# A fused attention and experts kernel: where half of a key's product stands, and which engine makes the second batch's x sums

## The chip, the cores and the metric

The kernel runs on one core of a Trainium2 chip, in one launch. The metric is the device time of that core in microseconds (us). Engines are named as the profile names them: PE is the tensor engine (PEld its loading of weights), DVE the vector engine, ACT the scalar engine, POOL is GpSimd, SP the engine that issues nearly all DMAs. Everything is computed in fp32.

## The reference

The input x is 2 batches of 2048 tokens with 512 features. One layer of gated delta-rule attention with 16 heads of 128, and a mixture of experts on the first 512 rows:

```python
q = silu(conv4(x @ Wq)); k = silu(conv4(x @ Wk)) * 128 ** -0.5; v = silu(conv4(x @ Wv))
alpha = sigmoid(x @ Wa + ba); beta = sigmoid(x @ Wb + bb)
def step(S, (qt, kt, vt, at, bt)):                      # per token and head
    err = S @ kt - vt
    S = at * S - bt * outer(err, kt)
    return S, S @ qt
o = layernorm(scan(step)) * ln_w + ln_b
attn = (o * sigmoid(x @ Wg)) @ Wo
# experts: 16 of them, 4 per token, weighted and added
expert = (silu(x @ gate.T) * (x @ up.T)) @ down.T
```

conv4 is a causal convolution over four tokens, one filter per feature. Both parts read the layer norm of the input, and the output is the input plus both.

## The kernel before

**Units and blocks.** The work is cut into 16 units u: batch u // 8 and one pair of heads. A unit runs over 4 blocks of 512 tokens, each of 4 chunks of 128. Inside a chunk the recurrence is solved with the inverse of a triangular matrix, whose small pieces come from an "inverse" per unit (L251 to L282; its steps are two operations each, L268 and L271): it loads a tile Y, works in it, copies to a tile X and stores both. Tiles X and Y are one buffer each.

**Seven products instead of eight.** Projections of the recurrence use sums of quarters of x and of the weights, so that seven products of half size do for eight. The sums of x are made once per block by `combine` (L526 to L545): four subtractions of 128x512 on DVE, and seven stores of 256 KB into `xs_d`. `x_part` (L790 on) loads them back as tiles `xr`, and the products are at L821.

**First stage** (to about 233 us). It normalises x, transposes it, makes the decays (`zaz`, alpha and beta), the keys of unit 0 and the first of unit 1, the routing of the experts and inverse 0. The order on PE, DVE, ACT and POOL is the order in which the code is written; SP's DMAs are placed by the scheduler. Ahead of a loop the first batch is handled; sixteen memsets on POOL (L438 and L439) zero operand tiles at the very start. The loop (t from 3) then does, for t = 3 to 10, two chunks of the second batch each:

- `turned` (L492 to L506), twice: four PE transposes of 128x128 (L505) and one ACT copy (L506);
- `gated` (L508 to L516): PE products for the gates (L513) and an ACT copy into zr (L516);
- `spread` (L518 to L524): two small transposes (L523) of zr;
- `scaled` (L482 to L490): the normalisation of the next two chunks, on ACT for the second batch (L486); `moments` (L463 to L480): statistics on DVE and a power on POOL (L476);
- every second time `combine(1, g)`, with its sums on DVE.

Between these stand the steps of a pipeline of keys, one key (a head of a block) per t. `key_item` (L399 to L422) has the product in two halves (`proj_part`, L184, two matmuls of 128x512 each), the copy into `raw` and the last tap on ACT (`conv_taps`, L148 to L160), three taps on DVE (`conv_sum`, L166), and silu on ACT (L420). Behind the second half of a unit's last key the weights of the next unit are asked for (`load_wk`). Scores of older keys (`scores`, L228), their decays (`dec_start` L211, `dec_run` L219) and `put_a` (L232) follow. The routing (`route`, L1633 to L1687) gives steps in some turns of the loop.

```python
if first:
    turned(1, n1)
...
key_step(t), key_step(t)
if first:
    gated(1, n1)
```

**Recurrence** (`recurrence(b)`, L1106 on). For every chunk the code writes out a hand-made order: products of the next block's q, v, g and k, the chunk's own work, and the experts' work, whose gathers (L1696) are issued by POOL. POOL also makes the next unit's inverse, three steps in every chunk, from chunk 2 of a unit's first block on. Behind inverses 2 to 5, in u = 1 to 4, it makes sums of the output weights, `wo_sums` (L1248 to L1268): loads into tile Y, four subtractions of 128x256, two stores, twice in a unit. Everything on POOL runs in order, also L995 and L997 (the chunk's kv path), L920 (qg, 128x512) and L1080 and L1081 (rs and nb of the output norm), for which ACT's L1094 waits.

Of the kernel before, what the change touches and what calls it, by code (L numbers as in the profile page):

```python
# [45 lines left out]
def block_kernel(ctx, tc, x, wq, wk, wv, wg, wo, wa, wb, ba, bb, par, consts,  # L46
# [59 lines left out]
            for p in range(3)]  # L106


    xs_d = [[dp.tile([P, 7, 2 * TH], F32, name=f"xs_d{b}_{k}") for k in range(NBK)] for b in range(NB)]

    a_d = [dp.tile([H, NC * DW], F32, name=f"a_d{b}") for b in range(NB)]
    gin_d = [dp.tile([H, T], F32, name=f"gin_d{b}") for b in range(NB)]
# [322 lines left out]
             for k, n in (("a32", C), ("ilo", Q), ("ihi", C), ("top", 3 * Q), ("bot", C), ("a64", C))}  # L435
            for i in range(2)]
    invs = [opp.tile([P, HG, C], F32, tag=f"inv{i}", name=f"inv_{i}") for i in range(4)]
    for t in [*ops[0].values(), *ops[1].values(), *invs]:  # L438
        nc.gpsimd.memset(t, 0.0)  # L439

    with ExitStack() as es:
        mp = es.enter_context(tc.tile_pool(name="moe", bufs=2))
# [83 lines left out]
        def combine(b, g):  # L526

            if b > 0:
                first, second = xts[b, g * CB], xts[b, g * CB + 2]
            else:  # L530
                first, second = x0[g][:, :, 0:TH], x0[g][:, :, TH:]
            b11, b21, b12, b22 = first[:, 0:2], first[:, 2:], second[:, 0:2], second[:, 2:]
            eng = nc.vector

            def new():
                return bp.tile([P, 2, TH], F32, tag="v", name="t", bufs=4)

            t1, t2, t4 = new(), new(), new()
            eng.tensor_tensor(t1, b12, b11, ALU.subtract)
            eng.tensor_tensor(t2, b22, t1, ALU.subtract)  # L540
            eng.tensor_tensor(t4, b21, t2, ALU.subtract)
            t3 = b12 if b > 0 else new()
            eng.tensor_tensor(t3, b22, b12, ALU.subtract)
            for i, t in enumerate((b11, b21, t2, t1, t3, t4, b22)):
                nc.sync.dma_start(out=xs_d[b][g][:, i, :].rearrange("p (k t) -> p k t", k=2), in_=t)  # L545
# [102 lines left out]
        with tc.manual_schedule(engines={E.PE, E.DVE, E.Activation, E.Pool}):  # L648
            moments(0, 0, 1), moments(0, 1, 2)
            for g in range(NBK):  # L650
                for c in range(g * CB, (g + 1) * CB):
                    scaled(0, c)
                    if c + 2 < NC:
                        moments(0, c + 2, c + 3)
                    if c % 2 and g + 2 < NBK:
                        fetch(0, g + 2, (c % CB // 2,))
                    turned(0, c)
                    if c > 1:
                        (spread(0, c - 3) if c > 2 else None) if c % 2 else gated(0, c - 2)
                if g == 1:  # L660
                    key_step(0), key_step(0)
                if g > 1:
                    combine(0, g - 2)
                if g == 2:
                    key_step(0)
            gated(0, NC - 2)
            nc.vector.tensor_scalar(lnh, prm[:, 3 * H * (KS + 1):], 0.5, None, ALU.mult)
            d0, d1 = decays(0), decays(1)
            fetch(1, 0), fetch(1, 1)
            combine(0, 2)  # L670
            key_step(1)
            spread(0, NC - 2)
            next(d0)
            key_step(1), key_step(2), key_step(2)
            moments(1, 0, 2)
            next(d0), next(d0)
            ask(0, 0, 0), ask(0, 0, 1)
            key_step(1)
            key_step(0)
            next(d0), next(d0)  # L680
            key_step(2)
            drain(d0)
            scaled(1, 0), scaled(1, 1)
            key_step(1), key_step(0)
            combine(0, 3)
            moments(1, 2, 4)
            n1 = 0
            r = route(nc, any_bank, mp, cst, cstf[:, N_CONST * P:], topk_idx, topk_w, tw, pos, wrow, trow)
            inv, firsts = iter(()), []
            def first_inverse():  # L690
                yield from inverses(0, nc.vector)
                load_ops(0)

            for t in range(3, len(keyed) + 2):
                first = t < 11
                old = t - 3
                if t == 11:
                    loads(0)
                    firsts = [item(0, what, h, later)
                              for what, h in (("q", 0), ("v", 0), ("q", 1), ("v", 1), ("g", 0), ("g", 1))]  # L700
                if t == 11:
                    inv = first_inverse()
                    next(inv)
                p = firsts[t - 11] if 0 <= t - 11 < 6 else iter(())
                p1 = firsts[t - 12] if 0 <= t - 12 < 6 else iter(())

                if first:
                    turned(1, n1)
                done = keyed[old][0] < 2
                if done:  # L710
                    dec = dec_start(*keyed[old])
                key_step(t - 2)
                if done:
                    pk = bank(ps_l, "l") if old < 8 else any_bank()
                    scores(pk, kts.pop(keyed[old]))
                if first:
                    turned(1, n1 + 1)
                else:
                    next(d1, None)
                key_step(t), key_step(t)  # L720
                if first:
                    gated(1, n1)
                next(p, None), next(p, None)

                key_step(t - 1)
                if done:
                    dec_run(dec, *keyed[old])
                    put_a(pk, dec, *keyed[old])
                key_step(t)
                next(p1, None), next(p1, None)  # L730
                next(p, None)
                if first:
                    spread(1, n1)
                    n1 += 2
                    nxt = n1 // CB + 1
                    if n1 < NC:
                        scaled(1, n1), scaled(1, n1 + 1)
                    if n1 + 2 < NC:
                        moments(1, n1 + 2, n1 + 4)
                    if n1 % CB == 0:  # L740
                        combine(1, n1 // CB - 1)
                    if n1 % CB and nxt + 1 < NBK:
                        fetch(1, nxt + 1)
                for _ in range({4: 1, 5: 1, 6: 2, 7: 1, 8: 1, 9: 1, 10: 2}.get(t, 0)):
                    next(r)
                for _ in range(8):
                    next(inv, None)
                next(p1, None)
                saves()
            drain(d1, r, inv)  # L750
# [355 lines left out]
    def recurrence(b, pending):  # L1106
# [20 lines left out]
        with tc.manual_schedule(engines={E.PE, E.DVE, E.Activation, E.Pool}):  # L1127
# [8 lines left out]
            for m, at in enumerate([*steps, None, None]):  # L1136
# [4 lines left out]
                if at:  # L1141
# [10 lines left out]
                    if c == 2 and blk == 0:  # L1152
                        drain(inv)
                        inv = inverses(u + 1, nc.gpsimd) if u + 1 < NB * NP else none
                        if 0 < u <= H // 4:
                            inv = chain(inv, wo_sums(2 * u - 2, 2 * u - 1))
                        step(inv)
                    a = before(n, c)
                    what = (PLAN if n + 1 != n0 + (NP - 2) * NBK else "qvgk")[c]
# [88 lines left out]
    def wo_sums(*rows):  # L1248

        for i in rows:  # L1250
# [15 lines left out]
            nc.sync.dma_start(out=wo_d[:, 0, i, :], in_=t)  # L1266
            nc.sync.dma_start(out=wo_d[:, 1:, i, :], in_=w[:, 1:])
            yield  # L1268

    def chain(*gens):  # L1270
        for g in gens:
# [542 lines left out]
```

## Time and profile before

| | |
|---|---|
| median of 3 runs | 3609.84 us (3609.67 to 3609.89) |
| the profiled execution's own time | 3617.36 us |
| its span, first to last instruction | 3615.6 us |
| mean granted clock of PE | 0.989 |
| busy PE, DVE, ACT, POOL | 97%, 71%, 57%, 59% |
| moved by DMA | 714.60 MB |
| first product of the recurrence (L821) starts | 232.93 us |

The profiled execution took 7.52 us more than the median of the runs, so times from its trace add up to 3617.36 and not to 3609.84. PE is busy in 97% of the span, and the chain that ended last runs through PE for 83% of it. An average over the span hides the first stage: there PE is busy in 12 to 19 of every 20 us. "Granted clock" is the share of full speed that PE's throttle allowed. In a row of a timeline the number in brackets is the engine's idle time ahead of the instruction, with what ended it.

### The profile page before, as it was taken

Reading aid. Unit: us, or ns where it says so; the run is one execution under the profiler, and the core shown is the slowest. Engines: PE = TensorE matmul, PEld = TensorE weight load, DVE = VectorE, ACT = ScalarE, POOL = GpSimd, SP = SyncE. Lnnn points to the kernel's source line nnn. Section 1 sums busy time; section 2 is a strip of 40 time slices with the busy share of each in tenths; the row PEclk is TensorE's granted clock in tenths of the full one; section 3 lists DMA queues with packets and bytes.
Section 4 is the critical chain, followed back from the end, with each engine's and each line's share of the span. In section 5 each row is a group of like instructions: output and inputs, shape, how many; then the busy total and the mean of one; then the engine's idle time right before and its main releaser. Section 6 shows DMA issues by size and latency. Waiting matters only on the chain.

```text
span 3615.6 us, 69975 instructions
## 1 busy us (share of the span) xinstructions
PE 3500.4 (97%) x21604; PEld 3122.7 (86%) x21604; DVE 2562.0 (71%) x6468; ACT 2063.2 (57%) x5491; POOL 2127.2 (59%) x3680
## 2 busy tenths in 40 slices
PE   7889999999999999999999999999999999999999
PEld 4459888888888888889898889999999999899888
DVE  7777766767776777678784368888888888667532
ACT  4556555555655565666671047777767777666410
POOL 2137768677785777768661047666675858484200
PEclk9999999999999999999999999999999999999999
DMA  8667767768677687777787547575757576654432
GB/s 278 214 182 216 240 186 246 207 200 262 193 244 213 190 268 192 245 209 235 207 240 235 158 131 202 155 212 163 211 170 213 160 205 170 196 169 146 143 111 90
DMA packets 675652, 714.60 MB, mean 198 GB/s; under 512 B 364304, under 2 KB 469008, under 8 KB 675280
## 3 DMA queue, kind: packets, MB, share of 16 engines
q1 hardware_dynamic: 653168, 628.71, 59.5%
q0 software_dynamic: 22112, 81.41, 7.2%
q8 instruction: 175, 2.87, 0.3%
q14 instruction: 197, 1.61, 0.2%
HBM read 504.72 MB, written 205.13 MB: 196 GB/s over the span
## 4 chain that ended last, share of the span: by engine, by line
PE 83%; DMA 4%; DVE 3%; POOL 2%; ACT 2%; issue 1%; SPq 0%; POOLq 0%; DVEq 0%; ACTq 0%
PE y L821 21%; PE z L821 16%; PE z L1318 5%; PE p L1730 4%; PE l L967 3%; PE p L1318 3%; PE y L1318 3%; PE c L1049 3%; PE c L1040 3%; PE o L1064 3%; PE o L1067 3%; PE c L1029 3%; PE p L228 2%; PE p L1747 2%; PE l L1000 2%; PE l L982 2%
## 5 line engine op out<-in xcount | busy, mean ns | idle before, releaser
L911 DVE SCALAR_TENSOR_TENSOR cv<-raw,prm,cv 128x512 f32<-128x512 f32 x1086 | 934.4, 870 | 11.6 <-ACT cv L149 4.7
L995 POOL COPY inv<-iT 32x32 f32<-32x32 f32 x512 | 195.9, 383 | 378.0 <-DVE top L988 205.6
L826 ACT COPY e<-y 128x256 f32<-128x256 f32 x734 | 271.1, 369 | 240.2 <-PE y L821 233.7
L1080 POOL TENSOR_TENSOR rs<-rs,mhalf 128x2 f32<-128x2 f32 x256 | 181.6, 710 | 381.9 <-DVE nb L1079 379.4
L149 ACT ACTIVATE cv<-raw,prm 128x512 f32<-128x512 f32 x362 | 295.7, 817 | 108.1 <-DVE raw L887 108.1
L271 POOL TENSOR_TENSOR Y<-Y,t 128x30 f32<-128x30 f32 (+14 forms) x450 | 296.0, 658 | 35.2
L268 POOL TENSOR_TENSOR t<-Y 128x30 f32<-128x30 f32 (+14 forms) x450 | 280.1, 622 | 36.6 <-DMA gin<-gin_d 14.3
L1056 DVE SCALAR_TENSOR_TENSOR S<-S,gtot,c 128x128 f32<-128x128 f32 x480 | 145.0, 343 | 177.4 <-PE c L1049 176.9
L887 DVE TENSOR_TENSOR raw<-z,e 128x256 f32<-128x256 f32 x244 | 103.5, 424 | 230.1 <-PE z L821 229.0
L1102 ACT ACTIVATE oT<-c,lnh 128x256 f32<-128x256 f32 x256 | 144.2, 563 | 179.5 <-PE c L1099 168.8
L920 POOL TENSOR_TENSOR qg<-q,gin 128x512 f32<-128x512 f32 x126 | 192.2, 1525 | 72.2 <-DMA gin<-gin_d 46.7
L1094 ACT ACTIVATE o<-o,nb,rs 128x128 f32<-128x128 f32 x512 | 202.4, 444 | 45.3 <-POOL nb L1081 44.1
L821 PE MATMUL y<-xr,wq 128*128 128x256 f32 x756 | 197.7, 385 | 15.8 <-DMA xr<-xs_d 15.5
L1103 POOL TENSOR_TENSOR oT<-g,oT 128x256 f32<-128x256 f32 x256 | 192.0, 750 | 29.0 <-ACT oT L1102 28.6
L821 PE MATMUL y<-xr,wg 128*128 128x256 f32 x760 | 196.6, 381 | 5.7 <-DMA xr<-xs_d 5.7
L1064 PE MATMUL o<-w,pT 128*128 128x128 f32 x1024 | 194.8, 275 | 0.0
L821 PE MATMUL y<-xr,wv 128*128 128x256 f32 x756 | 194.5, 380 | 0.0
L1730 PE MATMUL p<-xgT,w 128*128 128x128 f32 x1488 | 181.4, 275 | 11.8 <-DVE aTf L232 7.5
L843 DVE TENSOR_TENSOR raw<-z,e 128x256 f32<-128x256 f32 x245 | 102.8, 420 | 123.5 <-ACT e L826 39.6
L1067 PE MATMUL o<-S,qg 128*128 128x128 f32 x960 | 185.7, 275 | 0.0
L1064 PEld LDWEIGHTS o<-w,pT 128*128 128x128 f32 x1024 | 173.3, 191 | 12.8
L1730 PEld LDWEIGHTS p<-xgT,w 128*128 128x128 f32 x1488 | 171.4, 182 | 14.5 <-DVE aTf L232 9.0
(335 smaller groups left out, 10187.6 us busy)
## 6 DMA issues: line engine op xcount, KB each, us to landing
xr<-xs_d SPq DMA_DIRECT2D x191, 512.0 KB
row<-a_d SPq DMA_DIRECT2D x128, 258.0 KB
dec_d<-decA SPq DMA_DIRECT2D x128, 258.0 KB
decB<-dec_d SPq DMA_DIRECT2D x64, 516.0 KB
gin<-gin_d SPq DMA_DIRECT2D x128, 256.0 KB
k_d<-kf SPq DMA_DIRECT2D x128, 256.0 KB
k<-k_d SPq DMA_DIRECT2D x64, 512.0 KB
aT_d<-aTf SPq DMA_DIRECT2D x128, 256.0 KB
```

Source lines behind the costliest of these rows:

```text
L149: nc.scalar.activation(cv, of, AF.Identity, bias=cbias(p, h0 + h), scale=tap(p, h0 + h, KS - 1))
L268: eng.tensor_tensor(t, bass.AP(col.tensor, col.offset, [col.ap[0], (Q, j), (0, n)]), bass.AP(row.tensor, row.offset, [row.ap[0], (0, j), ( ...
L271: eng.tensor_tensor(Y[:, 0:j, j + 1:], Y[:, 0:j, j + 1:], t, ALU.add)
L821: nc.tensor.matmul(ps[:, 0:TH], lhsT=a[i - 1][:, k, :], rhs=xs[j][:, slot, k, :], start=start and k == 0, stop=k == 1, skip_group_check=no ...
L826: nc.scalar.copy(e, py[:, 0:TH])
L911: nc.vector.scalar_tensor_tensor(cv, (r0, r1)[h][:, j:j + BLK], tap(p, u % NP * HG + h, j), cv, ALU.mult, ALU.add)
L995: nc.gpsimd.tensor_copy(inv[0:Q, h, Q:2 * Q], iT[r + Q:r + 2 * Q])
L1064: nc.tensor.matmul(po[:, h * D:(h + 1) * D], lhsT=pT[:, h, :], rhs=w[:, h, :], start=True, stop=S is None)
L1067: nc.tensor.matmul(po[:, h * D:(h + 1) * D], lhsT=qg[:, h, cs], rhs=S[:, h, :], start=False, stop=True)
L1094: nc.scalar.activation(o[:, h, :], po[:, h * D:(h + 1) * D], AF.Identity, bias=nb[:, h:h + 1], scale=rs[:, h:h + 1])
L1318: nc.tensor.matmul(ps[:, 0:TH], lhsT=a[0][h // 4][:, h % 4, :], rhs=W[w][h], start=start and h == 0, stop=h == n8 - 1, skip_group_check=no ...
L1730: nc.tensor.matmul(ps[:fn, s, :], lhsT=w[f][:, s, k, :], rhs=xt[:, k, :], start=(k == 0), stop=(k == NKT - 1))
```

## The change

Four edits go together.

1. `xs_d` of the second batch gets an eighth slot, and `combine(1, g)` only stores the four quarters of x, without sums: b11 in slot 0, b21 in slot 1, b12 in slot 7, b22 in slot 6.
2. A new `x_sums` makes the sums later, in the recurrence of the first batch, on POOL: it loads slots 0 and 1 into a tile of tag X and slots 6 and 7 into one of tag Y (512 KB each), lets three steps go by, subtracts four times and stores slots 2 to 5. It runs behind inverse 1 (blocks 0 and 1, in u = 0) and behind inverse 2 (blocks 2 and 3, in u = 1). The sums of the output weights move from u = 1 to 4 to u = 2 to 5.
3. The sixteen memsets move from the start to a place behind the first batch's last `combine` and `moments(1, 2, 4)`.
4. For t = 3 to 10 the first half of key t's product goes in front of the first `turned`, the second half behind the second `turned`; for later t the order stays.

```diff
-    xs_d = [[dp.tile([P, 7, 2 * TH], F32, name=f"xs_d{b}_{k}") for k in range(NBK)] for b in range(NB)]
+    xs_d = [[dp.tile([P, 7 + b, 2 * TH], F32, name=f"xs_d{b}_{k}") for k in range(NBK)] for b in range(NB)]
...
-    for t in [*ops[0].values(), *ops[1].values(), *invs]:
-        nc.gpsimd.memset(t, 0.0)
...
                 first, second = xts[b, g * CB], xts[b, g * CB + 2]
-            else:
-                first, second = x0[g][:, :, 0:TH], x0[g][:, :, TH:]
+                for t, lo in ((first[:, 0:2], 0), (first[:, 2:], 1), (second[:, 0:2], 7), (second[:, 2:], 6)):
+                    nc.sync.dma_start(out=xs_d[b][g][:, lo, :].rearrange("p (k t) -> p k t", k=2), in_=t)
+                return
+            first, second = x0[g][:, :, 0:TH], x0[g][:, :, TH:]
...
-            t3 = b12 if b > 0 else new()
+            t3 = new()
...
             moments(1, 2, 4)
+            for t in [*ops[0].values(), *ops[1].values(), *invs]:
+                nc.gpsimd.memset(t, 0.0)
...
                 if first:
+                    key_step(t)
                     turned(1, n1)
...
-                key_step(t), key_step(t)
+                key_step(t)
                 if first:
                     gated(1, n1)
+                else:
+                    key_step(t)
...
-                        if 0 < u <= H // 4:
-                            inv = chain(inv, wo_sums(2 * u - 2, 2 * u - 1))
+                        if u < 2:
+                            inv = chain(inv, x_sums(2 * u), x_sums(2 * u + 1))
+                        elif u < 6:
+                            inv = chain(inv, wo_sums(2 * u - 4), wo_sums(2 * u - 3))
...
+    def x_sums(blk):
+
+        lo, hi = (ap.tile([P, 2, 2, TH], F32, tag=tag, name="xh") for tag in "XY")
+        of = xs_d[1][blk]
+        for t, k in ((lo, 0), (hi, 6)):
+            nc.sync.dma_start(out=t, in_=of[:, k:k + 2, :].rearrange("p s (k t) -> p s k t", k=2))
+        for _ in range(3):
+            yield
+        b11, b21, b22, b12 = lo[:, 0], lo[:, 1], hi[:, 0], hi[:, 1]
+        nc.gpsimd.tensor_tensor(b11, b12, b11, ALU.subtract)
+        yield
+        nc.gpsimd.tensor_tensor(b12, b22, b12, ALU.subtract)
+        yield
+        nc.gpsimd.tensor_tensor(b22, b22, b11, ALU.subtract)
+        yield
+        nc.gpsimd.tensor_tensor(b21, b21, b22, ALU.subtract)
+        for k, t in enumerate((b22, b11, b12, b21)):
+            nc.sync.dma_start(out=of[:, 2 + k, :].rearrange("p (k t) -> p k t", k=2), in_=t)
+        yield
```

## The prediction

> **What bounds the kernel now.** I read the busy line of the page first, then a table of busy time by stretches, then the tensor engine's timeline where that table shows gaps.
>
> ```profile
> PE 3500.4 (97%) x21604; PEld 3122.7 (86%) x21604; DVE 2562.0 (71%) x6468; ACT 2063.2 (57%) x5491; POOL 2127.2 (59%) x3680
> ```
>
> The span is 3615.6 us, so PE idles 115 us in all. The stretches (columns: busy us of each engine, granted clock, DMA share, GB/s) tell where:
>
> ```profile
> core 0: us, PE busy (x) PEld busy (x) DVE busy (x) ACT busy (x) POOL busy (x), PEclk, DMA share, GB/s
> ...
> 80.00:100.00 20.00, 17.49 (x73) 10.54 (x70) 15.86 (x34) 11.47 (x24) 3.22 (x8) 0.91 0.88 288
> 100.00:120.00 20.00, 14.80 (x65) 8.92 (x65) 18.98 (x42) 11.47 (x24) 3.36 (x6) 0.91 0.92 293
> 120.00:140.00 20.00, 16.00 (x63) 9.05 (x62) 13.93 (x24) 10.12 (x22) 3.35 (x7) 0.87 0.70 202
> ...
> 220.00:240.00 20.00, 12.29 (x55) 9.29 (x55) 12.56 (x18) 8.20 (x23) 7.27 (x11) 0.83 1.01 319
> ...
> 420.00:440.00 20.00, 20.00 (x125) 17.43 (x124) 15.93 (x40) 12.85 (x31) 11.65 (x22) 1.00 0.74 178
> ```
>
> In the first stage (to 233 us) no engine is full: PE 14.8 to 17.5 of 20, and POOL, with 3, nearly free. In the recurrence PE is full (20.00 of 20), so there only a new PE wait costs. PE's timeline shows one period of the loop over t (start, duration, line, operation, and in brackets the idle time before it and its cause):
>
> ```profile
> 126.41 0.66 PE L505 MATMUL c<-unit,xn 128*128 128x128 f32 x4 [1.55 <-ACT xn L486]
> 126.90 1.06 PE L228 MATMUL l<-kf 128*128 128x128 f32 x8
> 127.79 1.02 PE L505 MATMUL c<-unit,xn 128*128 128x128 f32 x4
> 128.60 4.92 PE L184 MATMUL p<-x,wk 128*128 128x512 f32 x8
> 133.45 1.92 PE L513 MATMUL l<-xt,wab 128*32 128x256 f32 x8
> 135.82 0.31 PE L523 MATMUL o<-unit,zr 32*128 32x32 f32 x2 [0.45 <-ACT zr L516]
> 137.67 0.77 PE L505 MATMUL c<-unit,xn 128*128 128x128 f32 x4 [1.54 <-ACT xn L486]
> ```
>
> PE and ACT take turns: after `gated` (L513) PE waits 0.45 us for zr and 1.55 for xn, while ACT runs zr 0.36, the key's raw copy 0.57, cv 0.77 and xn 0.75. Undisturbed periods are 9.57 us (74.08 to 83.65, 94.76 to 104.33): 5.35 from transposes to `gated`, 1.91 of `gated`, 2.31 of ACT.
>
> **The change part by part.** *Half product in front.* Two of the four matmuls of 128x512 (half of 3.60 us: 1.8) come before the transposes, and 0.45+1.55 = 2.0 us of idle time can hold them. ACT's chain then sets the head of the next period at 2.6 after `gated`'s end; from there `gated` starts after 3.55 (two transposes, scores, the other half, ACT's copies), then 1.91: 8.06 instead of 9.57, or 1.5 less. Period by period, each by the head (first L505) before and worked out after:
> - t=3 and 4 (60.81, 74.08, 83.65): 1.5 each, 0 if something else holds.
> - t=5 (83.65 to 94.76): routing matmuls of 1.8 us fill part of the gap: 0.8 (0 to 1.55).
> - t=6: key 7 takes the bank that the routing holds until a DVE copy (L1652, ended 105.89), some 8.5 after the head; its half product must wait: 0.8 lost.
> - t=7: key 8 begins unit 1, whose weights are fetched only behind key 7's second half. That load was issued at 112.71 and landed at 118.5; PE waited 1.20 for it. In front of the transposes it is needed sooner: head after 11.6 instead of 9.57, 2 lost (0.2 to 2.1).
> - t=8 (12.51 long, with that 1.20 and slow-clock matmuls): 3.5 gained (2.7 to 4.4). t=9 (11.26): 2.6 (2.0 to 3.2). t=10, head 137.67 to `gated` 144.67: 2.7 (1.95 to 3.45).
>
> Sum 9.8 (6.5 to 14). The spread is the clock: the scores (L228) take 1.06 or 1.91 us, and the 100 to 140 us rows grant 0.91 and 0.87.
>
> Behind the gaps the granted clock falls: 0.69 in 85 to 88 us, 0.57 in 115 to 118, 0.50 in 128 to 130, 0.59 in 139 to 142. The Trainium skill ("TensorE: Matmul & The Clock Gate", sections "HAM oscillation" and "Part 4: PE-mode transpose") has the clock halve after some 3.4 us without matmuls, transposes not counting as such. By it a half product in the gap ends the slow phases, for an estimated 4 us more; I don't count it.
>
> What follows `gated` is a chain: routing, DVE (95% busy 153 to 206: inverse 0 and keys), the last key, a store of aT_d (5.15 us), a load, and
>
> ```profile
> 232.93 2.05 PE L821 MATMUL y<-xr,wq 128*128 128x256 f32 x4 [7.71 <-DMA xr<-xs_d]
> ```
>
> All of it moves with `gated`. Inverse 0's input lands about when it is wanted; I take 0.3 off.
>
> *Sums off DVE.* 16 subtractions at 0.69 us (11 us) and 12 of 28 stores of 256 KB leave the first stage. No step of the chain above waits for them, so: 0. Without this, DVE in 100 to 120 (18.98 of 20) would be late next, so it keeps the loop's gain possible.
>
> *Zeros later.* 16 memsets hold POOL 5.8 us, to 6.52; the first rs (L476) runs at 6.57 though its input was ready at 4.40: 2.1 us at most. Behind it, waits for stores and for input (2.79, 1.78, 3.46 us at 14.43, 27.93, 43.77) take back about half: 1 (0 to 2.1). At the new place, near 66 to 72, POOL's own next step is a key's halo copy that is not late: 0, at worst 1.
>
> First stage: 9.8 - 0.3 + 1 = **10.5 gained** (6 to 15).
>
> *Sums on POOL.* Per block 2 loads of 512 KB, 4 subtractions, 4 stores of 256 KB; blocks 0 and 1 in u=0, 2 and 3 in u=1. POOL's subtraction of this size doesn't appear; its product L920 does, 1.26 to 1.77 us (mean 1.53): 16 x 1.53 = 24 us, beside 8 us idle in each 20 (11.65 busy at 420). Work is thus hidden; waits are not, as POOL runs in order, and behind a waiting subtraction stand L995 and kg (kv path) and rs and nb (L1080, L1081), for which ACT's L1094 waits, and for ACT's copy PE. The same happened in before, when inverse 3 waited for its input:
>
> ```profile
> 932.03 0.24 POOL L268 TENSOR_TENSOR t<-Y 128x30 f32<-128x30 f32 x1 [7.64 <-DMA gin<-gin_d]
> ```
> ```profile
> 936.73 0.81 ACT L1094 ACTIVATE o<-o,nb,rs 128x128 f32<-128x128 f32 x2 [2.98 <-POOL nb L1081]
> ```
> ```profile
> 937.85 0.92 PE L821 MATMUL y<-xr,swg 128*128 128x256 f32 x3 [1.07 <-ACT e L826]
> ```
>
> 7.64 us of POOL are 2.98 of ACT and 1.07 of PE; 6.66 us at 708.77 were 1.01 of ACT and none of PE directly, but 2.78 of PE later, for a late xr. So the first 6 us are nearly free. The sums' waits:
> - u=0, first block. The low load goes into tile X, which is free only when inverse 1's store (issued 404.41) has landed, near 408.5; the high one is issued near 413, lands near 419.5, and POOL arrives at 413: wait about 6, nb some 4.3 late, PE 2 (0 to 5). Second block: SP waits 3.6 for the first one's stores, xr later: 0.5 (0 to 2).
> - u=1, first block, in place of the wo sums, whose wait was short:
>
> ```profile
>   DMA ws<-in_wo: 4.9, 3
> ```
>
>  (2.49 of it at 634.0.) Now the high half, issued near 633.4, lands at 639.7 while POOL arrives at 631.5: wait 8.2, PE 2 (0 to 4).
> - Start of u=2: inverse 3's input loads queue on SP behind the stores; wait 8.5 instead of 6.66: 1 (0 to 4).
> - u=5, now with wo sums: 0.5 (0 to 3). u=2 to 4 exchange like for like.
>
> Recurrence: 2 + 0.5 + 2 + 1 + 0.5 = **6 lost** (0 to 20). The end of 0 is the idle rows; the end of 20 lets every wait through whole. I lean to the low side by the 6.66 and 7.64 rows.
>
> These waits are loads of 512 KB at 6 us each, as wk's 5.72 in this trace. The Trainium skill ("DMA: Bandwidth & Descriptors", "Anatomy of one DMA") has 2.0 us plus bytes at 436 GB/s, an estimated 3.2; by it each wait is 2.5 shorter and the loss about 2. The measured rows decide.
>
> Net: 6 - 10.5 = -4.5. The profiled execution, 3617.36 (span 3615.6), becomes 3612.9; the median, 7.5 below it throughout, goes from 3609.84 to **3605.3**.
>
> **The rivals.**
> A, my forecast: 3605.3, own range 3602 to 3610.
> B, the sums fit in POOL's idle time: loss at most 2, loop gains 10 to 15, perhaps with the clock up: 3609.84 - 12 + 1.5, about 3599. For it: 8 idle us in 20, and 6.66 us that PE hardly felt. Against it: X and Y are each one tile, so loads wait for stores.
> C, slower: the high half's load holds POOL in both u=0 and u=1, and inverse 3's input too. It decides once POOL's wait passes some 7 us (1.07 of PE at 7.64, and from there 1 for 1 as nb falls behind): 5 + 4 + 4 at the three places, 2 for xr, 3 for u=5 = 18, minus 8 of gain: 3620. For it: 2.78 of PE at 738.73 for xr behind such a wait. Against it: DMA share is 0.74 at 420, not 1.
> D, the half product gains nothing, held by bank and weights at t=6, 7 and by the routing at t=5: the loop gains 3, recurrence loses 6, start gives 1: 3611.8. For it: ACT's chain, not PE, ends each gap.
>
> **How the numbers follow.** A measurement of this kernel can tell about 0.2%, 7.2 us, from no change. A 0.43, B 0.35, C 0.14, D 0.08. A lies within 0.2%, D too, but for 0.01 each on the faster and the slower side: faster 0.36, same 0.49, slower 0.15. The likeliest is A: 3605.3. To hold 8 in 10 the range takes B down to 3596 and the nearer half of C, up to 3618.
>
> **What would show it.** The period of the transposes falls to near 8.1, no [1.55 <-ACT xn] before them, and the heads at t=7 and 8 stand apart by over 11 with PE or its loads waiting for wk. The first wq product comes near 222.5. Near 413 and 632, and at the start of u=2, POOL idles 6 to 8 before the subtractions, ACT's L1094 waits for nb, and PE idles behind. It is wrong if the first product hardly moves (D), if POOL's subtractions wait under 4 (B), or if PE loses over 12 after 400 us (C).

## The result and the profile after

The changed kernel is slower: 3634.28 us (median of 6 runs, 3628.0 to 3641.26) against 3609.76 (6 runs, 3607.13 to 3613.42), a ratio of 1.0066 with a 95% interval of 1.0053 to 1.008. The forecast was 3605.3, within 0.2% of before, with a range of 3596 to 3618. The profiled execution took 3640.83 us, with a span of 3639.0; the first one of before had 3615.6.

First the line of busy times and the stretches of the changed kernel, as for before (busy us of each engine, granted clock, DMA share, GB/s):

```profile
PE 3508.1 (96%) x21604; PEld 3126.1 (86%) x21604; DVE 2567.4 (71%) x6452; ACT 2064.0 (57%) x5491; POOL 2151.2 (59%) x3696
```
```profile
80.00:100.00 20.00, 16.77 (x75) 9.65 (x76) 17.34 (x45) 13.54 (x28) 4.37 (x11) 1.00 0.94 303
100.00:120.00 20.00, 14.95 (x57) 8.78 (x56) 12.34 (x23) 8.43 (x19) 1.36 (x3) 0.83 0.58 190
120.00:140.00 20.00, 18.64 (x87) 10.09 (x86) 14.07 (x23) 12.80 (x28) 5.66 (x11) 1.00 0.83 205
...
420.00:440.00 20.00, 16.51 (x87) 13.56 (x86) 16.44 (x28) 10.08 (x25) 16.40 (x25) 0.91 0.79 251
```

PE's work is the same. Of the 23 us by which the span grew, 16 are more idle time of PE and 8 are longer busy time, at a slower clock (0.987 for 0.989). In the loop PE is fuller (18.64 of 20 at 120 us, 16.00 before), but a stretch of the recurrence that was full now has 16.51, at a granted clock of 0.91.

Shares of a whole span can't tell where 23 us went. Both kernels issue the same 21604 matmuls, so I matched PE's instructions in order and took the start of the same instruction after minus before. Each column is one execution against the first profile of before, in us; minus means earlier. The last is an experiment told below, whose recurrence has no such sums. The second profiles show how far one execution can be trusted:

| start in before | before, second profile | changed | changed, second profile | sums left out |
|---|---|---|---|---|
| 233 (first wq product) | -0.4 | -6.6 | -5.7 | -9.4 |
| 340 | -0.5 | -6.0 | -6.0 | -8.9 |
| 440 (sums of u = 0) | -0.7 | -0.1 | 1.9 | -8.8 |
| 630 | 1.9 | 0.2 | 2.5 | -9.1 |
| 700 (sums of u = 1) | 1.7 | 9.6 | 9.7 | -8.3 |
| 745 | -1.0 | 4.9 | 5.0 | -12.7 |
| 1575 | 2.8 | 2.0 | 5.6 | -11.6 |
| 1600 (end of u = 5) | 2.8 | 15.3 | 17.9 | -11.6 |
| 1880 | 3.7 | 18.7 | 20.3 | -11.6 |
| 3110 | 3.9 | 19.9 | 22.7 | -10.6 |
| 3604 | 7.9 | 23.7 | 29.6 | -12.2 |

So 6 us are gained in the first stage and lost in u = 0; u = 1 takes 9 against the column on the right (against before, 4.7 of them come back by 745, where before has a wait of its own); 13.2 go in 25 us at the end of u = 5; some 8 more behind that, where the second profile of before loses 5.

**The loop did what was forecast.** PE's timeline of the changed kernel, one period:

```profile
123.20 1.98 PE L184 MATMUL p<-x,wk 128*128 128x512 f32 x4
125.02 0.60 PE L503 MATMUL c<-unit,xn 128*128 128x128 f32 x4
125.45 1.06 PE L228 MATMUL l<-kf 128*128 128x128 f32 x8
126.35 0.60 PE L503 MATMUL c<-unit,xn 128*128 128x128 f32 x4
126.78 1.88 PE L184 MATMUL p<-x,wk 128*128 128x512 f32 x4
128.60 1.91 PE L511 MATMUL l<-xt,wab 128*32 128x256 f32 x8
130.97 0.31 PE L521 MATMUL o<-unit,zr 32*128 32x32 f32 x2 [0.46 <-ACT zr L514]
131.20 1.98 PE L184 MATMUL z<-x,wk 128*128 128x512 f32 x4
```

From half to half 8.0 us (123.20 to 131.20; 8.06 forecast), and the 1.55 us wait for xn is gone. Two lines of the same view show what takes part of it back, ahead of key 7 and ahead of key 8. The third is the first product of the recurrence, whose wait was 7.71 before:

```profile
99.61 1.96 PE L184 MATMUL y<-x,wk 128*128 128x512 f32 x4 [2.32 <-DVE cum L1679]
...
112.25 3.78 PE L184 MATMUL z<-x,wk 128*128 128x512 f32 x4 [4.60 <-DMA wk<-in_wk]
...
226.31 2.04 PE L826 MATMUL y<-xr,wq 128*128 128x256 f32 x4 [7.04 <-DMA xr<-xs_d]
```

Key 7's half waits for the bank that the routing holds, key 8's for the weights of unit 1, and behind those 4.60 us the four matmuls take 3.78 instead of 1.98.

**u = 0.** POOL waits before the first subtraction, ACT behind it for nb, PE behind ACT. One line each from the timelines of POOL, ACT and PE:

```profile
414.65 1.39 POOL L1286 TENSOR_TENSOR xh<-xh 128x512 f32<-128x512 f32 x1 [6.67 <-issue]
```
```profile
424.39 0.81 ACT L1099 ACTIVATE o<-o,nb,rs 128x128 f32<-128x128 f32 x2 [4.96 <-POOL nb L1086]
```
```profile
425.51 2.08 PE L826 MATMUL y<-xr,swk 128*128 128x256 f32 x4 [3.49 <-ACT e L831]
427.38 1.79 PE L826 MATMUL z<-xr,swk 128*128 128x256 f32 x4
```

The wait was forecast at 6, nb 4.3 late, PE 2. PE lost 3.49, and then 1.8 more, as these two groups took 2.08 and 1.79 us, where such a group takes 1.03 elsewhere; the granted clock was 0.50 from 425.5 to 428.9. For POOL's wait the profile names no cause here ("issue"). The second load of the sums was issued at 410.17, and in u = 1 the same kind of wait, 5.23 us, is put down to the loads of the sums.

**u = 1.** PE's two longest waits there, 2.46 and 2.22 us, are for expert weights that POOL gathers; before waits 0.53 us for such weights there and the kernel without sums 0.62. The first of them:

```profile
654.76 1.46 PE L1757 MATMUL p<-xgT,w 128*128 128x128 f32 x11 [2.46 <-DMA w<-in_ew,wrow]
```

**The end of u = 5.** POOL, PE and two of SP's issues, all of the changed kernel:

```profile
1586.77 1.26 POOL L925 TENSOR_TENSOR qg<-q,gin 128x512 f32<-128x512 f32 x1 [7.86 <-DMA gin<-gin_d]
...
1596.26 0.24 POOL L268 TENSOR_TENSOR t<-Y 128x30 f32<-128x30 f32 x1 [8.10 <-DMA Y<-aT_d]
```
```profile
1597.85 0.49 PE L1045 MATMUL c<-r,inv 128*128 128x128 f32 x2 [3.55 <-POOL inv L1000]
...
1602.11 2.07 PE L826 MATMUL y<-xr,swg 128*128 128x256 f32 x4 [2.37 <-ACT e L831]
```
```profile
1582.31 0.38 SPq L1274 DMA_DIRECT2D wo_d<-ws  x1
1588.31 1.38 SPq L259 DMA_DIRECT2D Y<-aT_d  x3
```

The same two instructions of POOL before:

```profile
1577.85 1.47 POOL L920 TENSOR_TENSOR qg<-q,gin 128x512 f32<-128x512 f32 x1 [0.99 <-DMA gin<-gin_d]
...
1579.88 0.75 POOL L268 TENSOR_TENSOR t<-Y 128x30 f32<-128x30 f32 x1
```

Two waits, one behind the other, where before had 0.99 for gin and none for Y. The last sum of the output weights ends at 1576.7; its store is issued at 1582.31, and SP issues nothing more until the loads into the same tile Y go out from 1588.31 on.

**The start.** First transposes at 5.80 instead of 7.76, but the fourth at 15.58 behind 2.37 us of idle time (15.30 and none before), and the granted clock of that stretch (PE's busy us, clock, DMA share, GB/s):

```profile
12.00:16.00 4.00, 1.63 (x9) 0.99 0.95 324
16.00:20.00 4.00, 3.64 (x13) 0.50 1.06 310
```

### The profile page after: what moved, and what is told of

It reads as the page before. It is cut to its first block, busy times and chain, and to the rows that moved or that the text cites. A ratio compares the mean times of both kernels' runs of the same rounds, so it can differ in the third digit from the quotient of the medians.

```text
span 3639.0 us, 69982 instructions
## 1 busy us (share of the span) xinstructions
PE 3508.1 (96%) x21604; PEld 3126.1 (86%) x21604; DVE 2567.4 (71%) x6452; ACT 2064.0 (57%) x5491; POOL 2151.2 (59%) x3696
## 4 chain that ended last, share of the span: by engine, by line
PE 82%; DMA 5%; DVE 3%; issue 2%; POOL 1%; ACT 1%; SPq 1%; POOLq 0%; DVEq 0%; ACTq 0%
PE y L826 21%; PE z L826 16%; PE z L1345 5%; PE p L1757 4%; PE l L972 3%; PE y L1345 3%; PE p L1345 3%; PE c L1054 3%; PE c L1045 3%; PE o L1069 3%; PE o L1072 3%; PE c L1034 3%; PE p L228 2%; PE p L1774 2%; PE l L1005 2%
## 5 line engine op out<-in xcount | busy, mean ns | idle before, releaser
L826 PE MATMUL y<-xr,wq 128*128 128x256 f32 x756 | 197.0, 383 | 15.3 <-DMA xr<-xs_d 14.4
L1757 PEld LDWEIGHTS p<-xgT,w 128*128 128x128 f32 x1488 | 174.5, 185 | 19.9 <-DVE aTf L232 11.6
L1002 POOL TENSOR_TENSOR kg<-kv,gd 128x256 f32<-128x256 f32 x256 | 172.2, 673 | 25.0 <-ACT bot L999 3.1
```

What stands on the lines that cost most here:

```text
L826: nc.tensor.matmul(ps[:, 0:TH], lhsT=a[i - 1][:, k, :], rhs=xs[j][:, slot, k, :], start=start and k == 0, stop=k == 1, skip_group_check=no ...
L1757: nc.tensor.matmul(ps[:fn, s, :], lhsT=w[f][:, s, k, :], rhs=xt[:, k, :], start=(k == 0), stop=(k == NKT - 1))
```

## The experiments

Two theories stood against each other. **P, places**: the loss sits at single waits, each with its queue (the start, the loads of the sums in u = 0 and u = 1, the store at the end of u = 5). **L, load**: sums, loads and stores in the recurrence cost wherever they stand. Kernels of one set share their runs of before, and each median is set against those, as the sets ran on different chips. Executions of one kernel spread over 10 to 20 us, so shifts of the trace, as in the table, tell more than medians.

**half_only.** Before with the order of the halves alone (the two hunks in the loop).

> The kernel before with one edit: for t = 3 to 10 the first half of the key's product stands in front of the transposes. The second batch's sums stay on DVE, the zeros at the start, the sums of the output weights in u = 1 to 4. Theory P (places): the change's cost lies at single places, each with a queue of its own (start of the kernel 2.7 to 3.2 us, the sums in u = 0 6.3, in u = 1 about 2, the sums of the output weights at the end of u = 5 12.7), and the loop's gain is real. Then this one keeps the loop's gain of the changed kernel (periods of 8.0 us; 11.3 us between the first transposes of t = 3 and the last gates) as far as DVE, with its 11 us of sums, lets it: the first wq product 6 to 9 us earlier than 232.93, and the median 6 to 9 us under before, 3601 to 3604. Rival L (load): the recurrence loses because it begins earlier or at another phase of the transfers; then the first product is early here too, but the time is no better than before.

Measured 3613.75 against 3613.81, ratio 0.9995 (0.9981 to 1.0008). Up to the gates of t = 6 PE is 10.45 us ahead, and at the transposes of t = 8 it is 5.9 behind (two waits on PE between, 5.05 us for the bank that the routing's DVE operation holds and 9.17 for the weights of unit 1); the first wq product is at 231.92. The forecast of 6 to 9 us was wrong: the order alone gains nothing while DVE has the sums. How much of that is the sums and how much these two waits, sums_left_out and half_t78 below show in part.

**zeros_only.** Before with the memsets moved.

> The kernel before with one edit: the sixteen memsets moved behind the first batch's moments. Theory P: the first normalised tile comes 2 us earlier, but the fourth still waits for the store of xn_d, near 14.9, so PE idles over 2 us before its transposes near 15.6; the granted clock falls to 0.5 in 16 to 20 us and the first stage is 2 to 3 us later: median 3611.5 to 3613. Rival: the late start in the changed kernel comes from other stores and loads placed by the scheduler, not from the zeros; then the first product stands at 231 to 233 and the time is 1 to 2 us under before.

Measured 3619.74, ratio 1.002 (1.0009 to 1.0031): slower by some 7 us (3 to 11), where 2 to 3 were forecast. Its profiled execution was its fastest one (3611.5) and shows no fall of the clock at 16 us, so this profile alone doesn't show the cause. Six other profiles of this study have late zeros too. With zeros at the start (12 profiles) DVE's first operation on the gates (L551) begins at 45.4 to 47.3; with late zeros at 46.7 here and at 48.1, 48.1, 48.5, 50.1, 50.3 and 50.4 in the others. The clock fell to 0.50 at 15 to 18 us in both profiles of the changed kernel and in three others with late zeros, and in none with early ones. The fourth tile waits for a store until 14.0 to 15.0 either way, so starting 2 us earlier only makes PE's idle time before its transposes longer: 0.8 to 2.7 us with late zeros, 0 to 1.4 with early ones. That this gap lowers the clock is likely, not shown: after_t78 fell to 0.50 behind 1.22 us, and early_zeros kept 1.00 behind 1.37.

**wo_later.** Before, with the output weights' sums in u = 2 to 5.

```diff
-                        if 0 < u <= H // 4:
-                            inv = chain(inv, wo_sums(2 * u - 2, 2 * u - 1))
+                        if 1 < u < 6:
+                            inv = chain(inv, wo_sums(2 * u - 4, 2 * u - 3))
```

> The kernel before with one edit: the sums of the output weights in u = 2 to 5 instead of 1 to 4, nothing else. Theory P: the end of u = 5 is a bad place for them, because the store of tile Y holds SP, and behind it stand inverse 7's loads, gin and the x parts of the other batch: two POOL waits of about 8 us near 1579 and 1588 and PE 10 to 13 later there, while u = 1 gets 2 to 5 us quicker: median 3615 to 3621. Rival L: the loss at the end of u = 5 comes of the shifted phase in the changed kernel; then this one is within 3 us of before.

Measured 3629.31, ratio 1.0042 (1.0028 to 1.0056): some 15 us (10 to 20) without any sum of x. In the profiled execution, the fastest of the six, PE falls 10.5 us back between 1575 and 1600 and ends 6.5 behind before. POOL's timeline there:

```profile
1576.37 1.77 POOL L920 TENSOR_TENSOR qg<-q,gin 128x512 f32<-128x512 f32 x1 [5.21 <-DMA gin<-gin_d]
...
1586.51 0.24 POOL L268 TENSOR_TENSOR t<-Y 128x30 f32<-128x30 f32 x1 [8.24 <-DMA Y<-aT_d]
```

The same pair of waits. This line of the change, which exchanges "like for like" by the prediction, is its dearest.

**early_zeros.** The changed kernel with the memsets at the start.

> The changed kernel with one edit undone: the sixteen memsets at the start again. Theory P: the start is as in the kernel before (first transposes at 7.76 us, no clock of 0.5 in 16 to 20), the first wq product 2.7 to 3.2 us earlier than 226.31, near 223.4, and the median 2.5 to 3.5 us under the changed kernel's 3634.28. Rival: the zeros are not what makes the start late, and the time is equal or up to 2 us longer.

Measured 3642.41 (4 runs), ratio 1.0081 (1.0055 to 1.0106), an interval that overlaps the changed kernel's. The start is as forecast (L551 at 46.5, no clock of 0.50 before 54 us), but the first wq product is at 226.11, not 223.4: t = 6 and 7 give back 11.6 us here (9.2 ahead of before at 100 us, 2.4 behind at 114) and 7.4 in the changed kernel, so the weights and the bank take what the start gains.

**after_ws_in_x** and **after_ws_u6.** The changed kernel; the second row of output weights in tile X, or the last two rows in u = 6.

```diff
-            w = ap.tile([P, 4, TH], F32, tag="Y", name="ws")
+            w = ap.tile([P, 4, TH], F32, tag="YX"[i % 2], name="ws")
```
```diff
-                        elif u < 6:
-                            inv = chain(inv, wo_sums(2 * u - 4), wo_sums(2 * u - 3))
+                        elif u in (2, 3, 4, 6):
+                            i = 2 * (u - 2 - (u == 6))
+                            inv = chain(inv, wo_sums(i), wo_sums(i + 1))
```

> The changed kernel with one edit: of the two rows of output weights that a unit sums, the second one lies in tile X instead of Y. Tile Y is then free long before the unit ends. Theory P (the end of u = 5 costs because inverse 7's loads into Y wait for the store of the last sums, hold SP, and with it gin and the other batch's x parts): the POOL waits near 1579 to 1596 (7.86 and 8.10) fall to under 5 in sum, PE loses under 4 us there instead of 12.7, and the median is 8 to 11 us under the changed kernel. Rival Q: gin is late because the scheduler put it behind other issues, not because of Y; then the 7.86 us wait stays and PE still loses over 8 us there.

> The changed kernel with one edit: the last two rows of output weights are summed in u = 6 instead of u = 5. Theory P: no sums end at u = 5, so the 12.7 us at 1584 to 1591 go; at the end of u = 6, where the other batch's x parts are loaded too, some of it may come back (0 to 8): median 5 to 12 us under the changed kernel. Rival L (a general load of POOL and transfers, wherever it stands): no gain, the same loss at the end of u = 6.

With tile X the Y wait is gone and the gin wait stays (8.52); PE loses 4.8 at the end of u = 5 instead of 13.2. So both theories of that place were half right: Y accounts for some 8, gin for the rest. Between 745 and 1150, though, PE loses 13 us that the changed kernel doesn't, three times at a late xr. Half of that comes back by 1300, and this execution, the fastest of four, ends 7.7 us ahead of the changed kernel's; but the times (3640.31, ratio 1.0084, 1.0057 to 1.0112) show no gain. With the sums in u = 6 the end of u = 5 costs nothing (3.7 at 1575 and at 1600), and 6 come back between 1750 and 1880, about the end of u = 6: 3630.09, ratio 1.004 (1.0024 to 1.0055).

**after_t78.** The changed kernel with whole products for t = 7 and 8.

```diff
+                early = first and t not in (7, 8)
-                if first:
+                if early:
                     key_step(t)
```

> The changed kernel with one edit: for t = 7 and 8 the key's whole product stands behind the transposes, as in the kernel before; the half in front stays for the other t. In the changed kernel PE waited 2.32 us before key 7's half for the routing's DVE operation on its bank and 4.60 us before key 8's half for the weights of unit 1, which also let the clock fall. Theory: the period at t = 6 to 7 goes from 10.4 back to 8 to 9.6 and that at t = 7 to 8 from 14.4 to 9.6 to 11; the first wq product is 3 to 6 us earlier than 226.31, and the median 3 to 6 us under the changed kernel. Rival: the weights' load is asked for behind key 7's second half anyway and DVE or ACT take over the wait; then under 2 us are gained.

The first wq product is at 221.43, 4.9 earlier, as forecast. The end is 3.0 earlier than in the changed kernel's first trace; 3637.58, ratio 1.0062 (1.0044 to 1.008): no gain that the times can tell.

**sums_left_out.** Before with the halves' order; the second batch's quarters are stored in all seven slots and not one subtraction is made for that batch.

> The kernel before with the half product in front and with the second batch's x sums left out altogether: all seven slots are stored, from the four quarters of x, but nothing is subtracted, on DVE or later. The sums of the output weights stay in u = 1 to 4, the zeros at the start. It shows what the change could win if its sums cost nothing. Theory P: the first stage is like the changed kernel's with early zeros (first wq product near 226, against 231.92 with the sums on DVE), and the recurrence is as before: median 5 to 8 us under before. Rival L (an earlier start of the recurrence is lost there whatever is done): first product near 226, the time within 2 us of before.

Measured 3609.72 against 3612.49, ratio 0.9986 (0.9974 to 0.9998). First product at 223.57, and the table's last column keeps those 9 us to the end: an earlier start isn't lost by itself, so that form of L falls. With this order of the halves it is also the bound: sums for nothing are worth 3 to 5 us in the times, 12 in its one trace.

**x_longer_waits.** The changed kernel with one block of x sums in u = 0 and one in u = 1, ten steps ahead of the first subtraction; two blocks in u = 2; the output weights in u = 3 to 6.

> The changed kernel with its sums dealt out otherwise: one block in u = 0 and one in u = 1, each with ten POOL steps instead of three between its loads and the first subtraction; blocks 2 and 3 in u = 2 as the changed kernel has them; the sums of the output weights in u = 3 to 6. Theory P (the cost of the sums is POOL's wait for the 512 KB loads, with the chunk's work queued behind it): POOL's waits before the first subtraction in u = 0 and u = 1 (6.67 and 5.23) are gone, and with them PE's 6 us near 427 and most of the 9 us between 630 and 700; both come back in u = 2, and the ends of u = 5 and u = 6 cost as known: median 0 to 8 us under the changed kernel. Rival L (the load of 16 subtractions, 8 loads and 16 stores on POOL, SP and the transfers costs, not the wait): PE loses 4 us or more in u = 0 and 5 or more in u = 1 though no subtraction waits.

The shift is -7.0 at 340, -7.1 at 475, -6.0 at 630 and -5.8 at 700: u = 0 costs nothing, u = 1 nothing, with no subtraction waiting. u = 2, with two blocks, costs 2.4 by 930, which tells nothing, as half_t78, without such sums, loses 4.4 there; the ends of u = 5 and 6 cost 9.4 and 6.8. 3632.27, ratio 1.0033 (1.0021 to 1.0045). For u = 0 and u = 1 theory P holds, with half the sums in each.

**half_t78, pool_first, pool_first_t78.** Before with the halves' order; with whole products at t = 7 and 8, with the sums on POOL but in the first stage, and with both. The one new line:

```diff
-            eng = nc.vector
+            eng = nc.gpsimd if b > 0 else nc.vector
```

> The kernel before with the half product in front for t = 3 to 10 except 7 and 8; sums on DVE in the first stage, zeros at the start, sums of the output weights in u = 1 to 4. It asks whether DVE's sums, or the waits for bank and weights at t = 7 and 8, took half_only's gain (first product at 231.92, only 1 us early, after 10.45 us were won up to t = 6). Theory W (the waits): without them the loop keeps 8 to 10 us, first wq product 222 to 226, median 5 to 9 us under before. Theory V (DVE, with its sums, is full and late): the first product stays at 229 to 232 and the median within 3 us of before.

> The kernel before with the half product in front, and the second batch's x sums made by POOL, but in the first stage, at the place where DVE made them; no loads, no work moved into the recurrence, zeros at the start. POOL is busy 3 of 20 us there; four sums of 1.3 to 1.5 us stand behind the next moments and ahead of the next key's halo copies. Theory: the first product is near 226 to 228 as with the sums left out (223.6), the recurrence as before, median 4 to 7 us under before and 25 to 30 under the changed kernel: the change's loss lies in where it put the sums, not in the engine. Rival: POOL in order holds rs and the halo copies by up to 6 us every second period, so the loop loses it again: first product 230 to 234, time within 3 us of before.

> As pool_first, and for t = 7 and 8 the key's whole product stays behind the transposes. In the changed kernel that moved the first product 4.9 us forward (226.31 to 221.43). Theory: first product 220 to 224, the recurrence as before, median 8 to 12 us under before, the fastest of all. Rival as in pool_first: POOL's order takes it back, or the waits at t = 7 and 8 were hidden anyway: no better than pool_first.

Medians 3614.61, 3615.66 and 3611.95 against 3615.94; ratios 0.9988 (0.9975 to 1.0001), 1.0 (0.9987 to 1.0014) and 0.9981 (0.9968 to 0.9993). First products at 228.31, 231.36 and 229.53: half_t78 lies between its two forecasts, pool_first came out as its rival said, and pool_first_t78 missed its 220 to 224. So the sums needn't leave the first stage, and POOL is no better a place there than DVE; the last kernel is faster than both kernels of the change, by its ratio some 7 us (2.5 to 11.6) under before. In all three PE waits 5.0 to 5.9 us at t = 8 for the weights.

**wk_act, wk_act_pool.** half_t78 and pool_first_t78, with unit 1's weights asked for by ACT.

```diff
+            eng = nc.scalar if (tag, u) == ("wk", 1) else nc.sync
-            nc.sync.dma_start(out=t, in_=wp)
+            eng.dma_start(out=t, in_=wp)
```

> half_t78 with one edit: the weights of unit 1 are asked for by ACT instead of SP, right behind the copy that follows key 7's product. In half_t78 key 7's product ends near 102, SP issues the load at 109.98 behind 8 us of other issues, and PE waits 5.92 us at 116.71. Theory W: the load is issued near 102 and lands near 108, PE's wait at t = 8 goes to 0 to 1, first wq product 3 to 6 us earlier than 228.31, median 7 to 11 us under before. Theory V (DVE's sums set the loop's end): key 8 starts earlier, but DVE's taps, scans and inverse hold the end where it was: first product 227 to 229, median 1 to 4 under before.

> As wk_act, with the second batch's sums on POOL in the first stage instead of DVE (pool_first_t78 with the load on ACT's queue). Theory W: first wq product 223 to 226 against 229.53, median 9 to 13 us under before, the fastest kernel of this study. Theory V': POOL's sums hold the halo copies and the powers, so the first product stays above 227 and the median is 4 to 7 under before.

3614.25 and 3612.42 against 3617.64, ratios 0.9988 (0.9977 to 0.9999) and 0.9986 (0.9976 to 0.9995); first products at 229.11 and 227.56. The edit did not take the wait away: ACT's issue itself waited, until 112.56 in wk_act, and with it the zr copy, 10.99 us by the profile for a store of k_d, so that PE waited 9.07 there. The figures fit the theories V and V', but the load came no earlier, so neither was put to the test: whether an earlier load would bring the forecast 3 to 6 us stays open.

**repaired.** Everything mended at once, the sums still in u = 0 and 1: five steps of waiting, two subtractions a step, output weights in u = 2 to 4 (three, three, two rows), and the loop of wk_act with early zeros.

> The changed kernel's idea, mended: sums on POOL in u = 0 and 1 as it has them, with five POOL steps instead of three between loads and subtractions and two subtractions a step; the sums of the output weights three, three and two rows in u = 2, 3 and 4, two subtractions a step; whole products for t = 7 and 8; zeros at the start; unit 1's weights asked for by ACT. Theory P (the losses are waits at their places): first product 217 to 222, PE loses under 3 us each in u = 0 and 1 and nothing at the ends of u = 5 and 6, median 5 to 14 us under before. Rival L (sums in the recurrence cost by their load): the first product is as early, but 10 us or more are lost by 1900 us and the median is no better than before.

It fell: 3637.24, ratio 1.0053 (1.0039 to 1.0067). The first product is 9.0 early and nothing is lost at 427 (-8.8 at 440), so the waits were mended. But 4.8 go between 440 and 475, 6 more by 600, 5 by 700, and 11 between 745 and 1300. PE's timeline at the first of these:

```profile
438.80 2.65 PE L1758 MATMUL p<-xgT,w 128*128 128x128 f32 x16 [2.27 <-DMA w<-in_ew,wrow]
```

That is a gather of expert weights, and POOL issues those. Against PE's own shift, the gathers of before's 435.6 and 444.0 are 3.9 and 4.9 us late in this kernel, the first of them behind a pair of subtractions that takes 2.9 us. The changed kernel has it too: the gather of 642.2 is 4.1 late, and PE waits 2.46 for it at 654.76. That speaks for L in this form: two blocks in a unit make POOL late for the gathers even when no subtraction waits. It is not all of the loss: between 440 and 475 wk_act_pool, whose recurrence has no sums of x, loses 3.4 us too, and the second profile of before 1.9.

**changed_again, before_again.** Both kernels profiled once more, one run each, 3646.74 and 3625.27 (one more run of before beside them: 3626.03).

> The changed kernel, unchanged, profiled a second time. If the steps after 1600 us belong to the kernel, PE's shift against the first profile of before grows by 8 to 10 us again between 1600 us and the end, at the same instructions; if they belong to the execution, it grows by another amount (0 to 6) or elsewhere. The end of u = 5 should cost 12 to 14 again, u = 0 and u = 1 together 13 to 16 against a kernel without sums; the start has a granted clock of 0.5 for 3.4 or 6.8 us near 16 again.

> The kernel before, unchanged, profiled a second time. Its shift against its first profile shows what one execution's trace can tell: under 3 us at every mark if the shifts of the other kernels may be read to that; up to 8 if not, since the times of its executions spread from 3603 to 3626 us.

The columns are in the table above. u = 0 (7.8), u = 1 (7.1) and the end of u = 5 (12.3) repeat in the changed kernel, as does the clock of 0.50 at 16 us. Before stays within 4 us of itself up to 3110 and 8 off at the end. From 1600 on the changed kernel lost 8.4 and 11.7 us, before 5.2 in its second profile: part of that is the execution's, and what the kernel's part is stays open.

## Why the prediction was wrong

In the first profiles PE gained 6.6 us up to the first product, where 10.5 were forecast, and lost 30.3 behind it, where 6 were: 13.2 at the end of u = 5 (0.5 forecast), 5.9 in u = 0 (2.5), 4.8 from 630 to 745 (3), 8.4 behind 1600 (nothing), and small sums of both signs.

- **Period of the loop**: right (8.0 for 8.06). Counted between first transposes, t = 5, 8, 9 and 10 gave 1.8, 3.3, 3.3 and 3.4 (0.8, 3.5, 2.6 and 2.7 forecast), and t = 3, 3.6 for 1.5, because its half product now stands ahead of the first transposes, where PE had idled for 2.17. t = 6 lost the 0.8 forecast. t = 7 lost 4.9 instead of 2. Loop 11.3 for 9.8.
- **Clock**: the skill's rule ("TensorE: Matmul & The Clock Gate", "HAM oscillation") was set aside for want of a row, and the runs settle it only in part. The changed kernel was granted 1.00 at 80 to 100 and 120 to 140 us, with the gaps filled (0.91 and 0.87 before); but early_zeros, with the same order, got 0.87 at 80 to 100, and zeros_only, with the old one, 1.00 in both. Behind long waits matmuls did run at about half speed: behind 4.60 us at t = 8, 3.49 at 425, and 3.55 at 1597.85, where 0.50 was granted from 1599.7 to 1606.5. The 3.4 us that the page names is no sharp bound in these runs: behind 2.15 us of waiting at 1588.67 the changed kernel was granted 0.51 from 1589.4 to 1592.9, and behind 3.63 in u = 0 early_zeros kept 1.00.
- **Zeros later, "1 (0 to 2.1)" gained**: wrong in sign. The loop's first transposes came 3.2 us later than before (0.1 earlier in early_zeros), and zeros_only is slower. The wait for the store of xn_d was in the working, as something that takes back half; that PE idles for 2.37 us ahead of it, with a clock of 0.50 from 15.9 to 22.7, was not.
- **Behind the gates, "0.3 off"**: 8.1 us at the gates were 6.6 at the first product; PE's wait for DVE's aTf near 204 grew from 1.70 to 3.40.
- **First stage, 10.5 gained (6 to 15)**: 6.6, inside the range partly by luck, as the loop gave 1.5 more and the zeros 4.2 less than forecast.
- **u = 0, "2 (0 to 5)" and 0.5**: 5.9. The wait and nb's delay were right to 0.7 us. The price was not: PE waited 3.49, not 2, and the clock added 1.8. The row of 937.85, 1.07 of PE for 7.64 of POOL, was taken where 7.64 us of POOL made ACT 2.98 late, 4.7 to spare; here 6.67 made it 4.96, 1.7 to spare. In early_zeros, where the clock stayed at 1.00, u = 0 cost 3.5.
- **u = 1 and the start of u = 2, "2" and "1"**: 9 in u = 1 against the kernel without sums, and nothing at the start of u = 2. POOL waited less than forecast (5.23 for 8.2); the late gathers, which the list of what stands behind POOL's wait lacked, held PE for 2.46 and 2.22.
- **"u=5, now with wo sums: 0.5 (0 to 3). u=2 to 4 exchange like for like"**: the step that failed. It cost 13.2 (10.5 in wo_later, alone; nothing in after_ws_u6, which has no sums there). The prediction read no row of u = 5. At the ends of u = 2 to 4 before has one POOL wait each with the same store ahead of it, 7.64, 8.56 and 7.54 us, and PE waits at most 1.2 right behind, so that price was carried over. The end of u = 5 differs: gin's load is issued some 6 us later there, against PE's own shift, and Y's loads behind the store of the sums make a second wait, 8.10 behind 7.86, before POOL has caught up.
- **Rival C** had the side and the mechanism, at 0.14 and with 18 us for 30. Its point of decision, 7 us of POOL, is no threshold: 6.67 and even 5.23 were enough here.
- **Behind 1600**: 8.4 us that the prediction does not have. The second profile of before loses 5.2 there; what the change adds stays open.
- **DMA loads**: the loads that POOL waited for were issued at 410.17 and 632.72 and had landed at 414.65 and 637.55, under 4.5 and 4.8 us each. The row I used gave 6. The skill's estimate ("DMA: Bandwidth & Descriptors", "Anatomy of one DMA") was 3.2: too short for the second, to whose landing the profile puts POOL's wait. The page fits that formula to DMAs that GpSimd issues; SP issued these.

## What to carry to other kernels

Price a wait on an in-order engine by all that stands behind it, the DMAs it issues included, and by the slack at that very place; a price from another place (937.85 here) is worth little. Before moving work to a "like" slot, read what the DMA queue holds there: the end of u = 5, where the loads of the other batch's x parts begin, was not like the ends of u = 2 to 4. A wait on PE can be paid twice, when the clock falls behind it: at 425 the wait took 3.49 us and the half speed behind it 1.8 more.

## What the runs showed that I had not expected

- Executions of one kernel on one chip spread from 3606.8 to 3625.63 us (23 runs of before). Two profiles of before stayed within 4 us of each other up to 3110, so a trace of one execution tells shifts to about 4 us, and medians of few runs tell little under 0.2%.
- Starting earlier can end later: with the first transposes 2 us earlier the granted clock was 0.50 for 3.4 to 6.8 us near 16 us in five of seven profiles, and in none of the twelve others.
- POOL's subtraction of 128x512 takes 1.25 to 1.73 us; DVE's takes 0.69.
